# A mixer's third buffer in a ring over batches, its variances from per-batch moments, and seven landing buffers for its output

## The chip, the cores and the metric

The kernel runs on one core of one Trainium2 chip. The metric is device time in microseconds (us) of one launch, from the first to the last instruction of the core. The times before are three runs: 5021.53, 5029.39 and 5036.27 us, median 5029.39. The profile is of one further execution, with a span of 5033.2 us; all times of single instructions below are counted from the start of that span.

## The reference

The input is x with 4 images of 384 channels and 64 x 64 points, float32. Four layers follow one another, each as `x = x + layer(groupnorm(x))`: an attention, a convolution with an 8 x 8 Fourier filter and a gate, a token-and-channel mixer, and a 7 x 7 dynamic convolution. The change lies in layer 2, the mixer, and at the start of layer 3. What they compute is this, with `_bn` a batch normalization over batch and space, and `x2` the input of layer 2 after its group norm:

```python
tok = _bn(kw[:, 0:1] * y3 + kw[:, 1:2] * y5 + y1, ar_g, ar_b)
gp = tok.mean(axis=(2, 3), keepdims=True)
gates = sigmoid(_bn(_pw(gelu(_bn(_pw(gp, cg_w1), ...)), cg_w2), ...))
tok = tok * gates
h1 = gelu(_bn(_pw(tok, cm_w1), cm_g1, cm_b1))     # 384 -> 768 channels
h2 = _bn(_pw(h1, cm_w2), cm_g2, cm_b2)            # 768 -> 384 channels
x = x + gate * (tok + h2) + (1 - gate) * x2
# layer 3 begins with a group norm of x, its mean and its maximum over space:
# these give one scale per image and channel (x_w), then a 7 x 7 convolution
```

`h1` and `h2` need statistics over all four batches before the first value can be normalized. That cuts the mixer into three passes over the data: the first matrix product, the second, and the sum with which layer 3 begins.

## The kernel before

Channels lie on the 128 partitions, in three groups j = 0, 1, 2 (NJ = 3); a batch of a group is a row of 4096 points, and it is worked in four blocks of 1024. A framework places the instructions: the program is written in one order, each engine gets a queue of its own that is kept in order, waits are put in for data and for buffers, and a scheduler sets the place of each instruction in its queue.

**The first pass, "e" (in `phase_ef`, L1356 to L1403).** Sixteen blocks, b = 0 to 3 outside and i = 0 to 3 inside. For each block the token tensor is loaded in three parts, one for each channel group. Groups 0 and 1 land in a tile `e_tok` that has two buffers. Group 2 lands in a slice of `z_`, a large tile that is otherwise unused in this pass; which slice is written out by hand, at L1359:

```python
at = i % 3 * 1024
t = [t01[:, 0], t01[:, 1], self.z_[:, at : at + 1024]]
```

All loads are issued from SyncE's queue (SP), each part in four pieces. DVE scales the parts in place (L1364), TensorE forms six outputs `h_s` of 1024 columns from them (L1379, 72 matmuls a block in the trace), ACT copies them to `e_h` (L1386), DVE takes `bn_stats` of them (L1388) and works out the rest of the sum, `e_x` (L1392, L1393), of which the third part again reads the slice of `z_`. Then ACT's queue writes `e_h` to DRAM as `hid` (L1403), once per block.

**The statistics of the first product (L1404 to L1407).** After all blocks, one `bn_aggr` per output group folds the 32 sets of moments into mean and variance (L1406), and `bn_scale_shift` turns them into a scale and a shift (Ln and Exp on ACT, L312 and L313, three small DVE operations, L322 to L324). ACT's Gelu of the next pass (L1422) waits for them.

**The second pass, "f" (L1410 to L1447).** The same sixteen blocks: `hid` is loaded, Gelu is applied, TensorE forms `h_m` (L1435, 72 matmuls a block), ACT copies it out, DVE takes `bn_stats`. The result goes to DRAM as `h2`, but for the last batch, which stays in `z_` (`h2_last`). At the end of each batch a `bn_aggr` per group gives the moments of that batch alone, `mvb` (L1447); they are needed for layer 3's mean. After all blocks a second `bn_aggr` per group folds all 32 sets (L1450), and `bn_scale_shift` follows.

**`over_batches` (L327)** folds moments of four batches into one mean and variance. Before the change it is called once, for the token statistics ahead of the first pass ("ar"): `bn_stats` and `bn_aggr` for each group (L333, L334), a reduction and one more operation (L336, L338).

**The start of layer 3 (`phase_g`, `x2_of`, L1592).** The batches go in the order 3, 0, 1, 2 and the groups in the order 1, 2, 0. For each, a row of `wx` (what the first pass left of the sum) is loaded into one of three row buffers `x` (L1604), and `h2` comes in four quarters of 1024 into buffers `g_h2` (L1610); batch 3 has its rows loaded ahead and its `h2` in `z_`. For each quarter ACT scales `h2` into PSUM (`x_m`, L1614), DVE adds it to the row (L1615), ACT squares the sum for the variance, and writes the squares over the quarter's buffer, so that this instruction (L1617) is the one that frees it, and DVE takes the maximum (L1618). Groups 1 and 2 are written back to DRAM from POOL's queue (L1625); group 0 stays and is worked on. After the three groups come the group norm and the small products that give the batch's scale (`gn_pg`, `gn_pv`, `xw_m` L1636, `xw` L1646, `gx_m`). The strips and box sums of the batch before are woven in between (`first_chunk`: `to_strips` L1678 to L1695, `boxes` L1748 to L1801); they end with the write of the row to `rest` (L1801), which frees its row buffer. All buffers of `g_h2` are of the tag `toep`, of which there are four. That tag and the tag `rest`, with three buffers of the same size, belong to the convolution that comes after.

**The convolution (`conv7`, L1700 to L1731)** is then 3072 matmuls of 128 columns, with the remaining strips and boxes woven in.

Of the kernel before, what the change touches and what calls it, by code (L numbers as in the profile page):

```python
# [21 lines left out]
F32 = mybir.dt.float32  # L22
AF = mybir.ActivationFunctionType
ALU = mybir.AluOpType
AX = mybir.AxisListType

B, C, H, W = 4, 384, 64, 64
N = H * W
NJ = 3
P = 128  # L30
# [196 lines left out]
class _Builder:  # L227
# [99 lines left out]
    def over_batches(self, name, mv):  # L327

        nc = self.nc
        st = self.sm([P, NJ, 6], f"{name}_st")  # L330
        m = self.sm([P, NJ, 2], f"{name}_m")
        for j in range(NJ):
            nc.vector.bn_stats(st[:, j, :], mv[:, j, :, 0])  # L333
            nc.vector.bn_aggr(m[:, j, :], st[:, j, :])  # L334
        within = self.sm([P, NJ], f"{name}_w")
        nc.vector.tensor_reduce(within, mv[:, :, :, 1], AX.X, ALU.add)  # L336
        var = self.sm([P, NJ], f"{name}_v")
        nc.vector.scalar_tensor_tensor(var, within, 1.0 / B, m[:, :, 1], ALU.mult, ALU.add)  # L338
        return m[:, :, 0], var

    def bn_of_four(self, name, z, g, b, func, out):

# [960 lines left out]
    def phase_ef(self, strips):  # L1303
        tc, nc = self.tc, self.nc
        with ExitStack() as ctx:
# [5 lines left out]
            ep = first.enter_context(tc.tile_pool(name="e_const", bufs=1))  # L1311
# [5 lines left out]
            a, c = self.bn_scale_shift("bn_ar", *self.over_batches("ar", self.mvt), self.vec("ar_g"), self.vec("ar_b"))  # L1317
# [12 lines left out]
            mv = self.sm([P, NJ, 2], "cg2_mv")  # L1330
            for j in range(NJ):
                nc.tensor.matmul(z[:, j], lhsT=cg2[:, j * P : (j + 1) * P], rhs=gh, start=True, stop=True)
                st = self.sm([P, 6], "cg2_st")
# [17 lines left out]


            st = ep.tile([P, 6, B * 8, 6], F32, tag="h_st", name="h_st")
            sums = cp.tile([P, NJ, B, 4], F32, tag="wx_sum", name="wx_sum")
            for b in range(B):
                for i in range(4):  # L1356
                    blk = slice(i * 1024, (i + 1) * 1024)
                    t01 = io.tile([P, NJ - 1, 1024], F32, tag="tok", name="e_tok")
                    at = i % 3 * 1024  # L1359
                    t = [t01[:, 0], t01[:, 1], self.z_[:, at : at + 1024]]  # L1360
                    for j in range(NJ):
                        for q in range(4):
                            nc.sync.dma_start(t[j][32 * q : 32 * q + 32], self.tok[4 * j + q, b, :, blk])
                        nc.vector.tensor_scalar(  # L1364
                            t[j],
                            t[j],
                            self.at[:, j, b : b + 1],
                            self.ct[:, j, b : b + 1],
                            ALU.mult,
                            ALU.add,  # L1370
                        )
                    x = io.tile([P, NJ, 1024], F32, tag="x", name="e_x1")
                    nc.sync.dma_start(x, self.x1[b][:, :, blk])
                    h = hp.tile([P, 6, 1024], F32, tag="h", name="e_h")
                    for o in range(6):
                        s = self.ps("h_s")
                        for v in range(2):
                            for j in range(NJ):
                                nc.tensor.matmul(  # L1379
                                    s[:, v, :],  # L1380
                                    lhsT=w1[:, j, o * P : (o + 1) * P],
                                    rhs=t[j][:, v * 512 : (v + 1) * 512],
                                    start=j == 0,
                                    stop=j == NJ - 1,
                                )
                        nc.scalar.copy(h[:, o, :], s.rearrange("p a b -> p (a b)"))  # L1386
                        for v in range(2):
                            nc.vector.bn_stats(st[:, o, 8 * b + 2 * i + v, :], h[:, o, v * 512 : (v + 1) * 512])  # L1388
                        if o % 2:
                            j = o // 2  # L1390
                            at = lambda v: v[:, j, b : b + 1]
                            nc.vector.tensor_scalar(x[:, j], x[:, j], at(self.gx), at(self.gn), ALU.mult, ALU.add)  # L1392
                            nc.vector.scalar_tensor_tensor(  # L1393
                                x[:, j],
                                t[j],
                                self.gate[:, b : b + 1],
                                x[:, j],
                                ALU.mult,
                                ALU.add,
                                accum_out=sums[:, j, b, i : i + 1],  # L1400
                            )
                    nc.gpsimd.dma_start(self.wx[b][:, :, blk], x)
                    nc.scalar.dma_start(self.hidden[b][:, :, blk].rearrange("o p n -> p o n"), h)  # L1403
            mv = self.sm([P, 6, 2], "h_mv")  # L1404
            for o in range(6):
                nc.vector.bn_aggr(mv[:, o, :], st[:, o].rearrange("p a b -> p (a b)"))  # L1406
            a1, c1 = self.bn_scale_shift("bn_h", mv[:, :, 0], mv[:, :, 1], self.vec("cm_g1"), self.vec("cm_b1"))  # L1407


            first.close()  # L1410
# [3 lines left out]
            st2 = cp.tile([P, NJ, B * 8, 6], F32, tag="h2_st", name="h2_st")  # L1414
            mvb = cp.tile([P, NJ, B, 2], F32, tag="h2_mvb", name="h2_mvb")
            for b in range(B):
                for i in range(4):
                    blk = slice(i * 1024, (i + 1) * 1024)
                    h = hp.tile([P, 6, 1024], F32, tag="h", name="f_h")
# [5 lines left out]
                    if b == B - 1 and 0 < i:  # L1425
                        j = self.x2_order[i - 1]
                        nc.sync.dma_start(self.x2_ahead[i - 1], self.wx[b][:, j])
                    for j in range(NJ):
# [3 lines left out]
                        for v in range(2):  # L1432
                            m = self.pm("h2_m")
# [11 lines left out]
                            nc.gpsimd.dma_start(self.h2[b][:, j, blk], out)  # L1445
                for j in range(NJ):
                    nc.vector.bn_aggr(mvb[:, j, b], st2[:, j, 8 * b : 8 * b + 8].rearrange("p a b -> p (a b)"))  # L1447
            mv = self.sm([P, NJ, 2], "h2_mv")
            for j in range(NJ):
                nc.vector.bn_aggr(mv[:, j, :], st2[:, j].rearrange("p a b -> p (a b)"))  # L1450
            a2, c2 = self.bn_scale_shift("bn_h2", mv[:, :, 0], mv[:, :, 1], self.vec("cm_g2"), self.vec("cm_b2"))


            self.mean2, self.neg2 = self.coef("mean2"), self.coef("neg2")
# [1 line left out]
            for j in range(NJ):  # L1456
                nc.vector.tensor_scalar(self.gh[:, j, :], self.gate, a2[:, j : j + 1], None, ALU.mult)
                nc.vector.tensor_scalar(self.g0[:, j, :], self.gate, c2[:, j : j + 1], None, ALU.mult)
                m = self.mean2[:, j, :]
# [132 lines left out]
    def x2_of(self, b):  # L1592


        nc = self.nc
        mv = self.sm([P, NJ, 2], "gn_mv")
        mx = self.sm([P, NJ], "max")
        for j in self.x2_order:
            at = lambda v: v[:, j, b : b + 1]
            if b == B - 1:  # L1600
                x = self.x2_ahead.pop(0)
            else:
                x = self.gx_tile("x2")
                nc.sync.dma_start(x, self.wx[b][:, j])  # L1604
            var, top = self.sm([P, 4], "x2_var"), self.sm([P, 4], "x2_max")
            for q in range(4):
                sl = slice(q * 1024, (q + 1) * 1024)
                if b < B - 1:
                    h = self.gt_p.tile([P, 1024], F32, tag="toep", name="g_h2", bufs=4)
                    nc.sync.dma_start(h, self.h2[b][:, j, sl])  # L1610
                else:
                    h = self.h2_last[:, j, sl]
                m = self.psum.tile([P, 1024], F32, tag="c", name="x2_m", bufs=2)
                nc.scalar.activation(m, h, AF.Identity, bias=at(self.g0), scale=at(self.gh))  # L1614
                nc.vector.tensor_add(x[:, sl], x[:, sl], m)  # L1615

                nc.scalar.activation(h, x[:, sl], AF.Square, bias=at(self.neg2), accum_out=var[:, q : q + 1])  # L1617
                nc.vector.tensor_reduce(top[:, q : q + 1], x[:, sl], AX.X, ALU.max)  # L1618
                yield None
            nc.vector.tensor_reduce(mx[:, j : j + 1], top, AX.X, ALU.max)  # L1620
            nc.vector.tensor_copy(mv[:, j, 0:1], at(self.mean2))
            nc.vector.tensor_reduce(mv[:, j, 1:2], var, AX.X, ALU.add)
            nc.vector.tensor_scalar(mv[:, j, 1:2], mv[:, j, 1:2], 1.0 / N, None, ALU.mult)
            if j:
                nc.gpsimd.dma_start(self.scratch["x2"][b][j], x)  # L1625
        r, gm, n, _ = self.norm_of_groups(mv, True)
# [5 lines left out]
        m = self.pm("xw_m")  # L1632
# [18 lines left out]
        m = self.pm("gx_m")  # L1651
# [180 lines left out]
```

## Time and profile before

| what | before |
|---|---|
| time, median of 3 (lowest to highest) | 5029.39 us (5021.53 to 5036.27) |
| span of the profiled execution | 5033.2 us, 47996 instructions |
| TensorE busy | 4607.7 us, 92% |
| DVE busy | 2729.0 us, 54% |
| ACT busy | 2108.7 us, 42% |
| POOL busy | 762.8 us, 15% |
| DMA | 723.30 MB, mean 144 GB/s |

How to read it: TensorE is the engine that is busy nearly all of the time, so the span is mostly a row of stages that TensorE fills, with gaps in which it waits. The busy share of the whole doesn't show the gaps. The page divides the span into 40 slices of 126 us and gives each a digit for the busy share. In TensorE's row the slices that the change concerns, from 3271 us on, read first 9 throughout the two passes of the mixer (3271 to 4152 us), then 6 5 6 around the start of layer 3, and 9 again in the convolution. "idle before, releaser" in a line is the time for which the engine stood still ahead of these instructions, and what it then went on after. "SPq", "ACTq" and "POOLq" are the queues that issue DMAs; the time in such a line is that of the issue, not of the transfer.

### The profile page before, as it was taken

How to read it: one execution, taken by the hardware profiler on the slowest of the kernel's cores; microseconds unless marked ns; L12 is line 12 of the kernel's file. 1: busy time of each engine (PE TensorE's matmuls, PEld its weight loads, DVE VectorE, ACT ScalarE, POOL GpSimd, SP SyncE). 2: the span in 40 equal slices, each digit the busy share in tenths (PEclk: the TensorE clock that was granted, in tenths of full speed). 3: DMA queues.
4: the chain of work that ended last, by engine and by line, in shares of the span. 5: the costliest groups of instructions: out<-in, count | busy, mean ns of one | idle time of the engine just before them, and what ended most of it. 6: DMA issues, size and time to landing. Idle time of an engine off the chain costs nothing. (4 is left out here: it accounts for less than half of the span.)

```text
span 5033.2 us, 47996 instructions
## 1 busy us (share of the span) xinstructions
PE 4607.7 (92%) x17875; PEld 2614.2 (52%) x17875; DVE 2729.0 (54%) x4480; ACT 2108.7 (42%) x2811; POOL 762.8 (15%) x568
## 2 busy tenths in 40 slices
PE   5999999999999999999988999699999996569999
PEld 2333444334443444435467888344444443558999
DVE  5322455644656445565867778544421114767775
ACT  4444344554445444445345665311133334652320
POOL 1000000000000000000035555000000000135543
PEclk8999999999999999999989999799999997569999
DMA  5210211110111101113259999766664433757876
GB/s 167 72 48 29 84 57 60 65 59 33 68 63 65 52 32 63 63 61 100 89 162 286 290 293 296 255 239 248 238 238 150 150 134 136 255 181 229 235 214 193
DMA packets 344919, 723.30 MB, mean 144 GB/s; under 512 B 22011, under 2 KB 172390, under 8 KB 337766
## 3 DMA queue, kind: packets, MB, share of 16 engines
q1 hardware_dynamic: 283032, 477.56, 30.4%
q0 software_dynamic: 33152, 136.60, 7.2%
q10 hardware_dynamic: 28494, 105.99, 5.4%
q8 instruction: 144, 2.36, 0.2%
q14 instruction: 97, 0.79, 0.0%
HBM read 432.48 MB, written 287.57 MB: 143 GB/s over the span
## 5 line engine op out<-in xcount | busy, mean ns | idle before, releaser
L749 PE MATMUL av<-probs,vt 128*128 128x512 f32 x2048 | 964.6, 606 | 0.0
L720 ACT ACTIVATE probs<-sc_s 128x1024 f32<-128x1024 f32 x512 | 500.9, 1021 | 788.1 <-PE av L749 781.5
L749 PEld LDWEIGHTS av<-probs,vt 128*128 128x128 f32 x2048 | 370.3, 192 | 468.1 <-issue 461.0
L1154 PE MATMUL conv_m<-toep,z 128*128 128x256 f32 x2304 | 522.2, 386 | 11.0 <-DVE toep L1135 6.8
L945 DVE SCALAR_TENSOR_TENSOR acc<-band,vecs,acc 128x512 f32<-128x512 f32 x708 | 496.7, 746 | 45.8 <-POOL band L906 40.0
L1435 PE MATMUL h_m<-f_h,cm_w_t 128*128 128x512 f32 x1152 | 496.4, 594 | 7.9 <-ACT f_h L1422 7.9
L1154 PEld LDWEIGHTS conv_m<-toep,z 128*128 128x128 f32 x2304 | 440.5, 193 | 73.1 <-DVE z L1087 4.9
L1379 PE MATMUL h_s<-e_tok,cm_w_t 128*128 128x512 f32 x768 | 367.4, 602 | 5.5 <-DVE e_tok L1364 5.5
L1435 PEld LDWEIGHTS h_m<-f_h,cm_w_t 128*128 128x128 f32 x1152 | 219.4, 191 | 284.9 <-issue 273.8
L1135 POOL TENSOR_TENSOR toep<-w,band 128x1536 f32<-128x1536 f32 x94 | 323.8, 3445 | 285.7 <-PE conv_m L1154 244.7
L1722 PE MATMUL conv_m<-toep,z 128*128 128x128 f32 x3072 | 366.4, 278 | 0.1
L1722 PEld LDWEIGHTS conv_m<-toep,z 128*128 128x128 f32 x3072 | 357.1, 194 | 0.5 <-issue 0.5
L712 PE MATMUL sc_s<-q,k 32*128 32x512 f32 x2048 | 297.8, 650 | 22.5 <-ACT probs L720 22.0
L868 PE MATMUL t_m<-w_in_t,xb 128*128 128x384 f32 x768 | 276.9, 495 | 2.7 <-DVE coef L885 1.6
L1386 ACT COPY e_h<-h_s 128x1024 f32<-128x1024 f32 x96 | 97.2, 1012 | 421.4 <-PE h_s L1379 421.4
L782 PE MATMUL proj_m<-xm,w_proj_t 128*128 128x512 f32 x576 | 265.9, 600 | 5.0 <-DVE xm L735 3.5
L1379 PEld LDWEIGHTS h_s<-e_tok,cm_w_t 128*128 128x128 f32 x768 | 148.1, 193 | 192.6 <-issue 185.6
L789 DVE SCALAR_TENSOR_TENSOR x_res<-proj_m,bn_c,x_res 128x512 f32<-128x512 f32 x96 | 71.8, 748 | 319.5 <-PE proj_m L782 316.5
L1388 DVE BATCH_NORM_STATS2 h_st<-e_h 128x6 f32<-128x512 f32 x192 | 123.4, 685 | 194.9 <-ACT e_h L1386 194.9
L1443 DVE BATCH_NORM_STATS2 h_st<-f_h 128x6 f32<-128x512 f32 x72 | 49.8, 694 | 323.1 <-ACT f_h L1442 323.1
L868 PEld LDWEIGHTS t_m<-w_in_t,xb 128*128 128x128 f32 x768 | 142.7, 191 | 138.8 <-issue 59.6
L1379 PE MATMUL h_s<-z,cm_w_t 128*128 128x512 f32 x384 | 198.0, 599 | 12.6 <-DVE z L1364 12.6
(369 smaller groups left out, 6285.1 us busy)
## 6 DMA issues: line engine op xcount, KB each, us to landing
d<-d_o ACTq DMA_DIRECT2D x96, 512.0 KB
c_d<-d SPq DMA_DIRECT2D x96, 512.0 KB
hid<-e_h ACTq DMA_DIRECT2D x16, 3072.0 KB
f_h<-hid SPq DMA_DIRECT2D x16, 3072.0 KB
x_in<-in_x SPq DMA_DIRECT2D x96, 256.0 KB
x_res<-in_x SPq DMA_DIRECT2D x32, 768.0 KB
xa<-x_res POOLq DMA_DIRECT2D x32, 768.0 KB, 3.7
xa_in<-xa SPq DMA_DIRECT2D x32, 768.0 KB
```

The costliest lines, as they stand in the source:

```text
L712: nc.tensor.matmul(s[:, g], lhsT=k4[32 * g : 32 * g + 32, c], rhs=q[i][32 * g : 32 * g + 32], start=True, stop=True,)
L720: nc.scalar.activation(p[:, h * 1024 : (h + 1) * 1024], s[:, 2 * h : 2 * h + 2].rearrange("p a b -> p (a b)"), AF.Exp, scale=0.25,)
L749: nc.tensor.matmul(av, lhsT=vt[:, 4 * c + v, :], rhs=p[:, v * 512 : (v + 1) * 512], start=c == 0 and v == 0, stop=c == 7 and v == 3,)
L782: nc.tensor.matmul(m, lhsT=self.w_proj[:, j, o * P : (o + 1) * P], rhs=xm[:, j], start=j == 0, stop=j == NJ - 1,)
L868: nc.tensor.matmul(m[:, 0:C], lhsT=xb[:, j], rhs=self.w_in[:, j, :], start=j == 0, stop=j == NJ - 1,)
L945: nc.vector.scalar_tensor_tensor(out, src(j, k), w, done, ALU.mult, ALU.add)
L1135: eng.tensor_tensor(t, self.w53[:, at : at + 192].rearrange("p (m n) -> p m n", n=8).unsqueeze(2).to_broadcast([P, 24, 8, 8]), band.rearra ...
L1154: nc.tensor.matmul(m[:, c * 256 : (c + 1) * 256], lhsT=self.z_[:, at : at + P], rhs=t[:, 12 * c + 4 * i : 12 * c + 4 * i + 4].rearrange("p ...
L1379: nc.tensor.matmul(s[:, v, :], lhsT=w1[:, j, o * P : (o + 1) * P], rhs=t[j][:, v * 512 : (v + 1) * 512], start=j == 0, stop=j == NJ - 1,)
L1388: nc.vector.bn_stats(st[:, o, 8 * b + 2 * i + v, :], h[:, o, v * 512 : (v + 1) * 512])
L1435: nc.tensor.matmul(m, lhsT=w2[:, o, j * P : (j + 1) * P], rhs=h[:, o, v * 512 : (v + 1) * 512], start=o == 0, stop=o == 5,)
L1722: nc.tensor.matmul(m[:, ch * P : (ch + 1) * P], lhsT=self.z_[:, at : at + P], rhs=t[:, 8 * c + 2 * i : 8 * c + 2 * i + 2].rearrange("p m a ...
```

## The change

Three edits:

1. The slice of `z_` for the third part goes round over all sixteen blocks: `(4 * b + i) % 3` in place of `i % 3`. Before, block 3 of a batch and block 0 of the next one had the same slice, 0. Now any three blocks in a row have three different ones.
2. The mixer's statistics come from the moments of each batch. In the first pass six `bn_aggr` of 8 sets stand at the end of each batch (the new tile `hmv`), and `over_batches` folds the four batches. In the second pass the per-batch moments were there already, and `over_batches` takes the place of the `bn_aggr` over 32 sets. `over_batches` itself is rewritten: no `bn_stats` and `bn_aggr` by group, but seven small operations on all groups at once (sum, scale, difference, square, add, sum, scale). It is also used for "ar", as before.
3. The quarters of `h2` in `x2_of` alternate between the tags `toep` (four buffers) and `rest` (three): seven buffers in all.

```diff
     def over_batches(self, name, mv):
-        for j in range(NJ):
-            nc.vector.bn_stats(st[:, j, :], mv[:, j, :, 0])
-            nc.vector.bn_aggr(m[:, j, :], st[:, j, :])
-        within = self.sm([P, NJ], f"{name}_w")
-        nc.vector.tensor_reduce(within, mv[:, :, :, 1], AX.X, ALU.add)
-        nc.vector.scalar_tensor_tensor(var, within, 1.0 / B, m[:, :, 1], ALU.mult, ALU.add)
+        nc.vector.tensor_reduce(mean, mv[:, :, :, 0], AX.X, ALU.add)
+        nc.vector.tensor_scalar(mean, mean, 1.0 / B, None, ALU.mult)
+        nc.vector.tensor_sub(d, mv[:, :, :, 0], mean.unsqueeze(2).to_broadcast([P, n, B]))
+        nc.vector.tensor_mul(d, d, d)
+        nc.vector.tensor_add(d, d, mv[:, :, :, 1])
+        nc.vector.tensor_reduce(var, d, AX.X, ALU.add)
+        nc.vector.tensor_scalar(var, var, 1.0 / B, None, ALU.mult)
...
-                    at = i % 3 * 1024
+                    at = (4 * b + i) % 3 * 1024
...
-            for o in range(6):
-                nc.vector.bn_aggr(mv[:, o, :], st[:, o].rearrange("p a b -> p (a b)"))
-            a1, c1 = self.bn_scale_shift("bn_h", mv[:, :, 0], mv[:, :, 1], ...)
+                for o in range(6):
+                    nc.vector.bn_aggr(hmv[:, o, b], st[:, o, 8 * b : 8 * b + 8].rearrange("p a b -> p (a b)"))
+            a1, c1 = self.bn_scale_shift("bn_h", *self.over_batches("h", hmv), ...)
...
-            for j in range(NJ):
-                nc.vector.bn_aggr(mv[:, j, :], st2[:, j].rearrange("p a b -> p (a b)"))
-            a2, c2 = self.bn_scale_shift("bn_h2", mv[:, :, 0], mv[:, :, 1], ...)
+            a2, c2 = self.bn_scale_shift("bn_h2", *self.over_batches("h2", mvb), ...)
...
-                    h = self.gt_p.tile([P, 1024], F32, tag="toep", name="g_h2", bufs=4)
+                    tag, bufs = (("toep", 4), ("rest", 3))[q % 2]
+                    h = self.gt_p.tile([P, 1024], F32, tag=tag, name="g_h2", bufs=bufs)
```

The scheduler places some instructions otherwise as a result. On SyncE's queue the loads of a block at a batch's start stand before in the order "one piece of `e_tok`, four of `z_`, seven of `e_tok`", and after in the order of all other blocks, "eight of `e_tok`, four of `z_`". At the start of layer 3, three quarters of group 2 move ahead of the first row load of batch 0. For group 0 of batches 1 and 2, three of the four quarters (q = 0, 2, 1) stand ahead of the row load of that group, where before all four stood behind it. TensorE takes the matmuls of a batch's first output in the same order as those of all others, two of `e_tok` and one of `z` for each half, where before the four of `e_tok` came first. Apart from that, and from the added and removed small operations, TensorE, DVE, ACT and POOL keep their orders but for exchanges of near neighbours, most of them from layer 3 on.

## The prediction

> **What bounds the kernel now.** I read the page first (TensorE 92% busy), then the table of busy times for the four stretches from the mixer on:
>
> ```profile
> core 0: us, PE busy (x) PEld busy (x) DVE busy (x) ACT busy (x) POOL busy (x), PEclk, DMA share, GB/s
> 3200.90:3725.70 524.80, 504.31 (x1153) 221.75 (x1153) 261.53 (x395) 102.82 (x103) 11.47 (x16) 0.98 0.63 237
> 3725.70:4222.70 497.00, 496.39 (x1152) 219.37 (x1152) 71.62 (x108) 163.11 (x191) 19.29 (x37) 1.00 0.39 146
> 4222.70:4513.60 290.90, 149.64 (x728) 135.57 (x729) 200.22 (x371) 192.68 (x272) 62.65 (x64) 0.58 0.63 225
> 4513.60:5033.20 519.60, 485.95 (x4174) 478.82 (x4172) 370.94 (x409) 119.22 (x203) 244.99 (x148) 0.98 0.73 217
> ```
>
> The rows are pass e, pass f, the start of layer 3, and the convolution. Passes e and f run the same number of matmuls of the same shape, yet e takes 28 us more: that is what to look for. The third row is no TensorE stage (half of the time idle, clock 0.58): there a chain through all engines sets the pace. The fourth is TensorE's again and simply starts when the third ends, so what any of the first three loses or gains should reach the end.
>
> Next, where e loses. The write of `hid` is issued once per block, so its spacing is the block's time. From the timeline of ACT:
>
> ```profile
> 3297.97 0.37 ACTq L1403 DMA_DIRECT2D hid<-e_h  x1
> 3328.87 0.37 ACTq L1403 DMA_DIRECT2D hid<-e_h  x1
> 3366.39 0.37 ACTq L1403 DMA_DIRECT2D hid<-e_h  x1
> 3397.29 0.37 ACTq L1403 DMA_DIRECT2D hid<-e_h  x1
> ```
>
> A block takes 30.90 us; the one from 3328.87 on, the first of batch 1, takes 37.52. The first blocks of batches 2 and 3 take 36.64 (3459.09 to 3495.73) and 37.75 (3588.43 to 3626.18); all others 30.90. The cause is in the timelines of SP, DVE and TensorE there:
>
> ```profile
> 3327.82 1.69 SPq L1363 DMA_DIRECT2D z<-tok  x4
> 3329.56 14.08 SPq L1363 DMA_DIRECT2D e_tok<-tok  x7
> ```
>
> ```profile
> 3334.26 0.81 DVE L1364 TENSOR_SCALAR z<-z,at,ct 128x1024 f32<-128x1024 f32 x1 [4.11 <-DMA z<-tok]
> ```
>
> ```profile
> 3335.13 2.07 PE L1379 MATMUL h_s<-z,cm_w_t 128*128 128x512 f32 x2 [3.91 <-DVE z L1364]
> 3337.00 3.43 PE L1379 MATMUL h_s<-e_tok,cm_w_t 128*128 128x512 f32 x4
> ```
>
> The third part of a batch's first block can only be loaded when TensorE has done with the same slice, at the end of the block before. Its load, its scaling and a TensorE stop of 3.91 us follow; then six matmuls run at half speed (3.43 us for four, normally 1.88).
>
> For the third stretch, the group list with the scaling of `h2`, and ACT and SP around one such place:
>
> ```profile
> L1614 ACT ACTIVATE x_m<-g_h,g,gh 128x1024 f32<-128x1024 f32 x36 | 42.8, 1196 | 13.2 <-DMA g_h<-h 13.2
> ```
>
> ```profile
> 4373.66 0.32 SPq L1604 DMA_DIRECT2D x<-wx  x1
> 4374.07 5.95 SPq L1610 DMA_DIRECT2D g_h<-h  x4
> ```
>
> ```profile
> 4382.93 1.21 ACT L1614 ACTIVATE x_m<-g_h,g,gh 128x1024 f32<-128x1024 f32 x1 [3.25 <-DMA g_h<-h]
> 4387.67 1.21 ACT L1614 ACTIVATE x_m<-g_h,g,gh 128x1024 f32<-128x1024 f32 x1 [3.53 <-DMA g_h<-h]
> ```
>
> ACT waits 13.2 us in all for quarters of `h2`: 2.22 at 4290.81, the two shown, 3.00 at 4456.41 and 1.18 at 4466.11. The last four are in group 0 of batches 1 and 2, the group that ends the batch; its quarters are issued behind its row and share the DMA engines with it.
>
> **What the Trainium skill says.** "TensorE: Matmul & The Clock Gate", Part 1, states that an idle window of some 3.4 us drops the array to half its clock and that a busy one brings it back: the stops of 3.77 to 4.88 us are followed by matmuls at half rate in this trace, so a stop costs more than its idle time. "DMA: Bandwidth & Descriptors", section "Issuing engines are not separate DMA queues", says that all queues share the same 16 DMA engines: between 4374 and 4388 us a row of 2.1 MB and four quarters of 0.52 MB compete, as the 4.74 us between the two waits' ends shows. "VectorE: DVE Perf Modes", section on the TRN2 errata, says that each small operation pays a fixed cost: here dependent DVE operations on a few columns start 0.20 us apart (L322, L323, L324 at 3723.11, 3723.31, 3723.51).
>
> **The change part by part.**
>
> *The ring of `z_`.* With three different slices in a row, the load of a batch's first block may start two blocks earlier than now, as within a batch, where the trace shows no stop. The `e_tok` pieces, seven of which have stood behind that load in SP's queue, are freed as well. What is saved is the excess of the three blocks: 37.52 + 36.64 + 37.75 - 3 x 30.90 = 19.2 us. It is TensorE's own time with nothing beside it, so all of it counts. The DMA share in this stretch is 0.63, so earlier loads find room. Ends: 16 us if a smaller wait (row of `e_x`, `e_tok`) shows behind it, 19.2 if none. I take 19.2.
>
> *Statistics, pass e.* On the path are only the operations after the last `bn_stats` (3718.88, 1.28 us). Before: one `bn_aggr` of 32 sets, 1.02 us. After: one of 8 sets, 0.37 us by the row of L1447, then the seven operations of `over_batches`, each waiting for the one before, 7 x 0.20 = 1.4. So 1.77 against 1.02: +0.75 us, with ACT's Ln behind it and all of TensorE behind that. The 18 `bn_aggr` of earlier batches (18 x 0.37 = 6.7 us) lie on DVE, busy for half of this stretch; they are hidden.
>
> *Statistics, pass f.* The per-batch `bn_aggr` was there already. The last `bn_aggr` of 32 sets (0.96 us, 4223.76) goes, 1.4 us come: +0.45 us.
>
> *Statistics, "ar".* From 3184.75 to ACT's Ln at 3185.84 eight pipelined operations take 1.09 us; seven dependent ones take 1.4: +0.3 us. Sum of the three: +1.5 us. Ends: 0.8 if they start 0.1 us apart, as independent ones do in this trace, and 2.5 at 0.3 us (0.26 us is the longest of the small reductions, L1057).
>
> *Seven buffers.* Three quarters of a group ending a batch are now issued before its row, as soon as earlier quarters are squared. Then 0.52 MB instead of 2.1 MB compete with the row. Does a row get stuck behind a quarter that isn't free? In the order of the changed queue the quarter ahead of each row load needs a buffer freed by a square that also had to be done before (for example, the last one before the rows of batch 1, groups 2 and 0, needs the squares of group 1, done by 4348 us, and the row itself can't go before 4354.78). So no new wait. What may be saved: at 4290.81 about 2 us (the strips of batch 3 stand behind it on ACT). In group 0 of batch 1 the quarters are ready, and the adds (now from 4384.17 to 4395.3) are limited by the row and by ACT and DVE, about 2.3 us per quarter. With the row there at about 4381 they end at about 4391: 4 us. In batch 2, waits of 3.00 + 1.18, some of it replaced by the row's own arrival: 3 us. Sum 9 us. Bounds: 0, if the rows or DVE's queue come last everywhere, and about 16, the 13.2 us plus some gain for the rows.
>
> Sum: -19.2 + 1.5 - 9 = -26.7 us; 5029.4 - 26.7 = 5002.7, rounded to 5003 us.
>
> **The rivals.**
>
> *A, the early quarters bring nothing.* The chain of the third stretch goes through row buffers, POOL's writes and xw: DVE waits 25.6 us there for TensorE's `xw_m`, and POOL's write of a row stood behind an xw for 5.9 us. If these come last, only the ring counts: 5029.4 - 19.2 + 1.5 = 5012 us.
>
> *B, the early quarters bring more.* If each wait of 13.2 us is on the chain and rows land earlier too, 16 us or slightly more: 5029.4 - 19.2 + 1.5 - 16 = 4996 us.
>
> *C, the third stretch gets worse.* Quarters that are issued early compete with the rows that come last for two of the three batches, or an exchange of neighbours on POOL delays a write. At 5 us for each of three batches: 5012 + 15 = 5027 us, no measurable change. At double that, 5042 us, slower. For it speaks that DMA is at 0.98 in some of the 20 us windows there (4282 to 4302); against it that the bytes are the same and come out of just these windows.
>
> *D, the ring's gain is lost again*, because pass f or layer 3 wait for something other than TensorE. Against it: pass f's first Gelu waits for the last statistic of pass e, with nothing but TensorE's work ahead of it. It would give about 5020 us.
>
> **How the numbers follow.** Forecast (ring in full, 5 to 13 us from the buffers): 0.50. A: 0.22. B: 0.13. C: 0.08, of which 0.03 slower. D: 0.07. The bound of 0.3% is 15 us, so faster means below 5014: forecast, B and nearly all of A, as A is 2 us below it and the three runs before spread by 15 us: 0.50 + 0.13 + 0.20 = 0.83 and a little of D: 0.84. Slower 0.03. Same 0.13. The range takes in A and B with 3 to 6 us beyond them for the spread of medians: 4990 to 5016.
>
> **What would show it.** The spacing of `hid` in all sixteen blocks at 30.9 us, and no TensorE idle time put down to `z` in pass e, show the first step right. Pass e would then last about 506 us in place of 524.8, and the gap of TensorE between the passes, 7.88 us now, about 8.6. The stretch to the first matmul of the convolution, 290.9 us now, would be near 282 with ACT's wait for `g_h` under 3 us; at 290 with the wait gone, rival A is right. The prediction is wrong if one of the three batch starts still stops TensorE, or if the third stretch grows.

## The result, and the profile after

The changed kernel takes 5004.08 us (median of 4 runs, 5003.26 to 5010.24) against 5029.15 us before (4 runs, 5021.53 to 5036.27): the ratio is 0.9953, with a 95% interval from 0.9936 to 0.997. Five further runs of it, beside another 11 of the kernel before, gave 5011.48 us and a ratio of 0.9964 (0.995 to 0.9977). The profiled execution spans 5001.5 us, before 5033.2.

First the table of busy times by stage of the changed kernel, cut where the stages of the kernel before were cut, except that layer 3 begins with its first `x_m`: pass e, pass f with the statistics after it, the start of layer 3, the convolution.

```profile
core 0: us, PE busy (x) PEld busy (x) DVE busy (x) ACT busy (x) POOL busy (x), PEclk, DMA share, GB/s
3192.60:3697.66 505.06, 496.31 (x1152) 219.92 (x1153) 264.56 (x420) 102.80 (x103) 11.47 (x16) 0.99 0.66 246
3697.66:4200.17 502.51, 496.38 (x1152) 219.90 (x1152) 73.13 (x125) 166.09 (x196) 19.29 (x37) 0.99 0.40 148
4200.17:4472.90 272.73, 143.53 (x717) 129.04 (x718) 195.58 (x356) 188.88 (x264) 63.10 (x63) 0.59 0.65 234
4472.90:5001.50 528.60, 490.75 (x4186) 483.98 (x4184) 369.52 (x413) 119.75 (x206) 244.15 (x148) 0.97 0.72 213
```

With the same cuts the kernel before had 3200.9 us ahead of pass e, then 524.7, 502.0, 285.9 and 519.6. So in this pair of profiles 8.3 us went ahead of pass e, where hardly anything was changed, 19.7 in pass e and 13.2 at the start of layer 3; the passes' boundary costs 0.5 more, and the convolution is 9.0 us *longer*. The first of these five numbers says nothing of the change, and in those of pass e, of the start of layer 3 and of the convolution a part is chance, as the other profiles will show: one pair of executions isn't enough to read stages to a few us.

Pass e first. The writes of `hid` in the timeline of ACT, where batch 1 begins:

```profile
3319.22 0.37 ACTq L1405 DMA_DIRECT2D hid<-e_h  x1
3350.12 0.37 ACTq L1405 DMA_DIRECT2D hid<-e_h  x1
```

This is the block that took 37.52 us; it takes 30.90, and so do all others. In the list of what the engines sat idle for around `h_s`, no line with `z` is left (before, "DVE z" stood there with 27.6 us in 6 waits: three stops, each counted once for the matmul, together 12.6 us, and once for its weight load). The two waits for data that remain belong to the first block of the pass:

```profile
  DVE e_tok L1366: 6.1, 2
  DMA e_x<-x: 5.5, 1
```

The end of pass e, from DVE's timeline (start, duration, operation, and in brackets the idle time before it):

```profile
3691.34 0.37 DVE L1407 BATCH_NORM_AGGREGATE h_mv<-h_st 128x2 f32<-128x48 f32 x1
3691.75 0.18 DVE L332 TENSOR_REDUCE h_m<-h_mv 128x6 f32<-128x24 f32 x1
3691.96 0.17 DVE L333 TENSOR_SCALAR h_m<-h_m 128x6 f32<-128x6 f32 x1
3692.17 0.18 DVE L335 TENSOR_TENSOR h_d<-h_mv,h_m 128x24 f32<-128x24 f32 x1
...
3693.03 0.17 DVE L339 TENSOR_SCALAR h_v<-h_v 128x6 f32<-128x6 f32 x1
3695.09 0.17 DVE L322 TENSOR_TENSOR bn_h_a<-bn_h_a,vecs 128x6 f32<-128x6 f32 x1 [1.89 <-ACT bn_h_a L313]
```

The seven operations start 0.21 us apart. From the last `bn_aggr` to the first matmul of pass f is now 6.32 us, before 5.48; TensorE's gap between the passes is 8.72 us, where about 8.6 were foretold.

At the start of layer 3, the group of the scaling of `h2` in the list of groups:

```profile
L1614 ACT ACTIVATE x_m<-g_h,g,gh 128x1024 f32<-128x1024 f32 x36 | 42.8, 1195 | 0.0
```

ACT no longer waits for a quarter of `h2` at all; before, it was 13.2 us.

### The profile page after: what moved, and what is told of

The parts are those of the page before. It is cut to its first block, busy times and chain, and to the rows that moved or that the text cites. A ratio compares the mean times of both kernels' runs of the same rounds, so it can differ in the third digit from the quotient of the medians.

```text
span 5001.5 us, 48017 instructions
## 1 busy us (share of the span) xinstructions
PE 4589.6 (92%) x17875; PEld 2609.4 (52%) x17875; DVE 2728.0 (55%) x4508; ACT 2108.8 (42%) x2811; POOL 762.3 (15%) x568
```

## The experiments

Every run below stood beside runs of the kernel before on its chip, whose medians were 5028.14, 5028.22 and 5028.2 us. Single runs of one and the same kernel lie 7 to 26 us apart, so an edit of a few us has to be read from stages of many profiles, or from many runs.

**e1: the ring alone.**

```diff
-                    at = i % 3 * 1024
+                    at = (4 * b + i) % 3 * 1024
```

> Only the ring of the third token slice is changed. Theory 1 (the ring saves TensorE's stops at the three batch starts and nothing else): 19.2 us less than before, about 5010 us; pass e about 505 us long in place of 524.8, all blocks 30.9 us apart; the stretch from the last copy of h2 to the first matmul of the convolution and the convolution as before, 286 and 520 us, within the spread of one run to the next. Theory 2 (the gain is lost again behind it, as DMA or layer 3 wait for something else): less than 12 us. Theory 3 (the 8.3 us that the profile of the changed kernel is ahead of before when the mixer starts belong to the ring): pass e starts at about 3192 us here too.

5010.09 us, ratio 0.997 (0.996 to 0.998). All blocks take 30.90 us; pass e takes 505.4. The gain isn't lost afterwards, which answers the rival that it would be. What to compare it with is shown by the kernels that have no ring: their pass e took 524.7 us (before), 521.2 (e2) and 519.3 (e3), so the stops cost less in other executions than in the profile of before. Here the idle list around `h_s` of e3, the stops in place:

```profile
  DVE z L1364: 23.5, 6
  DMA hid<-e_h: 11.7, 1
```

23.5 us, where before had 27.6, counted in the same double way (TensorE itself stood still for 10.5 us and 12.6). In nine profiles with the ring pass e took 504.2 to 506.5 us, mean 505.5. The means differ by 16.2 us.

**e2: the statistics alone** (`over_batches`, the batch-wise `bn_aggr` of pass e, and the two calls, as in the change).

> Only the statistics are changed. Theory 1: 1.5 us more, that is no difference that can be measured; in the trace 0.8 us more between the last write of hid and the first matmul of pass f, 0.5 us more between the last copy of h2 and the first use of its scale, 0.3 us more ahead of the token scale. Theory 3 (the 8.3 us before the mixer come with the new small tiles or the new operations): 8 us less, with pass e starting at about 3192 us. If the start of pass e lies anywhere between 3190 and 3203 us without a pattern over these runs, the 8.3 us are the spread of code that the change doesn't touch.

5028.55 us, ratio 0.9998 (0.9989 to 1.0007): not to be told from no change. The chain is there all the same: 6.32 us from the last `bn_aggr` to pass f, as in each of the profiles with this edit that I read, and 5.48 in each without it.

**e3: the seven buffers alone.**

```diff
-                    h = self.gt_p.tile([P, 1024], F32, tag="toep", name="g_h2", bufs=4)
+                    tag, bufs = (("toep", 4), ("rest", 3))[q % 2]
+                    h = self.gt_p.tile([P, 1024], F32, tag=tag, name="g_h2", bufs=bufs)
```

> Only the seven buffers are added. Theory 1 (the stretch before the convolution gets shorter by some 13 us, and the convolution then takes some 9 us longer since its own loads and strips aren't there earlier): 4 us less than before, about 5025 us; the stretch about 273 us, the convolution about 528 us. Theory 2 (the longer convolution in the changed kernel's profile is chance): 13 us less, about 5016 us; the stretch 273 us, the convolution 520 us. Theory 3 (the shorter stretch is chance): no change, 286 and 520 us.

5025.24 us, ratio 0.9993 (0.9983 to 1.0003). The waits for `h2` are gone, the stretch to the first matmul of the convolution is 278.6 us, and the convolution takes 524.3. Pass e starts at 3202.0 us, so the 8.3 us ahead of it were not this edit's. The time, 2.9 us below its neighbours' median, is nearest to theory 1, but by itself it can't be told from no change.

**e4: ring and statistics, four buffers.**

> The changed kernel without the seven buffers. Theory 1: 17.7 us less than before, about 5011 us, with the stretch before the convolution at 286 us and the convolution at 520 us; the seven buffers are then worth about 4 to 7 us in the changed kernel. Theory 2 (the buffers bring their 13 us in full): the changed kernel is faster than this one by 13 us.

5011.3 us, ratio 0.9964 (0.9953 to 0.9976); pass e starts at 3199.9 us, and the start of layer 3 takes 286.5, as before. Theory 1's sum was right; the changed kernel is not 13 us faster than this one, so theory 2 falls.

**e5: the changed kernel again, unaltered.**

> The changed kernel again, unaltered, so that it stands beside the other runs on the same chip. Where the convolution's 48 sums are timed from the first x_m of layer 3, the four profiles without the seven buffers reach the fifth sum 348.7 to 354.7 us (spread 6) and the last at 797.9 to 803.3; the two with them at 343.7 and 348.7, and 796.3 and 797.8. Theory 1: the buffers are worth 4 to 5 us at the end and about 5 at the fifth sum; the 13 us of the first profile were partly chance. Then this profile has the fifth sum at 343 to 349 and the last at 794 to 799, and the median is 5003 to 5009 us. Theory 2: the first profile is typical, 9 us are won before the convolution and given back in it each time: fifth sum at 343 to 345, last at 796 to 797, median 5002 to 5005. Pass e starts anywhere from 3192 to 3203 (untouched code) under both.

5011.48 us. The fifth sum comes at 348.4 us, the last at 801.6 (the four profiles named there read 347.3 to 353.3 at the fifth). Theory 2 falls, since the first profile was not typical; theory 1's place for the fifth sum was met, its last sum and its median were missed by some 3 us on the slow side.

**e6: ring and seven buffers, old statistics.**

> Ring and seven buffers, the statistics as before. Theory 1 (the seven dependent operations stand on the path at two places that stop TensorE and once in the U-net): the gap from the last bn_aggr's start to pass f's first matmul is 5.48 us again (6.32 with the change), the one from the last aggr group to x_m 4.9 (5.5), and the time is 1 to 2 us below the changed kernel's, too little to be told from it by the medians. Theory 2 (aggregating by batch takes 18 operations off DVE's end and gains something elsewhere): the time is equal or 1 to 3 us longer.

5004.74 us, ratio 0.9958 (0.9945 to 0.9971). The chain is 5.48 us again. The times of e5 and e6 (5011.48 and 5004.74, 5 and 6 runs) can't be told apart by their ranges, 5004.96 to 5017.02 and 5000.28 to 5015.56.

**e7: the convolution's write of its sums one group later**, to see whether the order in SP's queue eats the head start.

```diff
         nc.vector.tensor_add(of, of, m)
-        nc.sync.dma_start(self.out[j][:, c0 : c0 + 8], o)
+        self.late = (self.out[j][:, c0 : c0 + 8], o)
...
         nc.sync.dma_start(o, self.rest[j][c0 : c0 + 8].rearrange("c y b n -> (y b) c n"))
+        self.write_late()
```

> The changed kernel with each write of the convolution's sums issued one group later, behind the next group's two loads, so that the strips' loads on SP's queue no longer stand behind a write that waits for DVE's sum of the same group. Theory 1 (what the convolution gives back is lost where TensorE waits for strips, and these stand in SP's queue behind the write): SP's wait for rest_o, 128 us in all, falls below 40, TensorE's waits for z, 20 us, fall below 8, and the time is 8 to 15 us below the changed kernel's. Theory 2 (the loads are paced by the DMA engines, at 0.8 to 0.94 there, and the queue's order is of no matter): the strips' loads take as much longer as they start earlier; the time is within 3 us.

5006.36 us, ratio 0.9956 (0.9943 to 0.997). SP's waits in the first 400 us of the convolution (line waited for, us in total, times, longest) of e7:

```profile
SPq L1702 <- DVE rest_o L1738: 119.2, 20, 11.2
```

They are nearly what they were (128.1 us in the changed kernel): SP simply arrives at the later write earlier and waits there. TensorE's waits for `z` stay too, at 20.3 us (20.5 in the changed kernel). Theory 1 falls.

**e8: the late write with the four buffers.**

> Ring and statistics with the four old buffers, and the late write of the sums. Theory 1 (the queue's order eats part of the head start): with the late write the seven buffers are worth more than without it, 7 to 10 us between this kernel and the one with late write and seven buffers, against some 5 without it. Theory 2 (the head start is lost to the DMA engines or was chance): 3 to 5 us between the two, as without it.

5011.22 us, ratio 0.9963 (0.995 to 0.9976): 4.9 us above e7, as theory 2 had it.

**e9: each box result written to `rest` in two pieces** (on e6: ring, seven buffers, old statistics).

```diff
+            if part == 3:
+                nc.gpsimd.dma_start(*rows(0, 24))
             for q in range(2):
...
-                nc.gpsimd.dma_start(self.rest[j][:, :, b], x.rearrange("p (y n) -> p y n", n=P))
+                nc.gpsimd.dma_start(*rows(24, 32))
```

> Ring and seven buffers with the old statistics (the kernel of e6), and each box result written to rest in two pieces, three quarters as soon as they are summed and the last quarter at the end, in place of 2.1 MB at the end. Theory 1 (what the convolution gives back is the wait of its first sum for the reload of rest, which stands behind the write of the last box result of the chunk: DVE waits 4.5 to 4.7 us there in every profile with the seven buffers and 1.8 in every one with four, SP 8.4 us for the write): the write that SP waits for falls from 8.4 to about 3 to 4 us, DVE's wait to under 1, TensorE's 4.2 us for the first sum go, the second sum comes 3 to 5 us earlier after the first x_m than in e6 (309.9) or its mean with seven buffers (313.6), and the time is 2 to 5 us below e6's. Theory 2 (the first sum waits for the DMA engines in general): the wait stays within 1 us and the time within 2 us.

4997.87 us, ratio 0.9936 (0.992 to 0.9952), five runs from 4989.58 to 5001.44: the fastest kernel of the study, below the changed one's 5004.08 and 5011.48. How it gains is only partly as theory 1 said. SP's wait for the write falls from 8.4 to 5.4 us, not to 3 or 4; DVE's wait for the reload is gone; but TensorE still waits 3.5 us for the first sum, and the second sum is only 0.6 us earlier than in e6. DVE's timeline of e9 ahead of that sum (L1731) shows why:

```profile
4502.21 3.65 DVE L1775 SCALAR_TENSOR_TENSOR box<-edge,off,box 128x128 f32<-128x128 f32 x1
4505.78 0.61 DVE L1776 SCALAR_TENSOR_TENSOR box<-in_x,off,box 128x384 f32<-128x384 f32 x1
...
4510.48 1.21 DVE L1710 TENSOR_TENSOR toep<-wmix,band_p 128x1024 f32<-128x1024 f32 x1
4511.61 1.21 DVE L1731 TENSOR_TENSOR rest_o<-rest_o,conv_m 128x1024 f32<-128x1024 f32 x1
```

The sum waits for no event: it stands in DVE's own queue behind box operations, one of which took ten times its usual 0.34 us. With the reload early, DVE became what comes last. From the convolution's first matmul to the third sum TensorE stands idle for 5.5 us, against 7.8 to 8.9 in the five profiles with seven buffers and whole writes. These 2.6 us below their mean are all of the gain that the traces place. The edit splits every box result's write, those inside the convolution too, and the profile of e9 reaches the end 795.1 us after the first `x_m`, that of e6 after 797.0: where the rest of the gain in the times comes from isn't shown.

**e10: the same write with the ring alone, four buffers.**

> The same writes in two pieces with the ring alone, four buffers (the kernel of e1). Theory 1: here DVE waits only 1.8 us for the reload and TensorE not at all, so the second sum moves by 1 to 2 us and the time by 0 to 2; the seven buffers are worth 2 to 4 us more between this kernel and e9 than the 3.8 us that they are worth without the split (all runs so far, fitted together). Theory 2: the two differ by some 4 us, as without the split.

5005.34 us, ratio 0.9956 (0.994 to 0.9971), nine runs from 4991.45 to 5017.88. At the medians this is 4.8 us below e1, and e9 is 6.9 below e6; the seven buffers are worth 7.5 us with it and 5.3 without (e1 to e6). The direction is that of theory 1, but runs of e10 spread over 26 us, and so this difference of differences is not shown. With the split TensorE waits 3.5 us for the first sum, as in e9, where e1 has no such wait. Its idle time from the first matmul to the third sum is 5.6 us, as without the split (5.4 to 5.9 in the five profiles with four buffers), and the profile reaches the end 804.9 us after the first `x_m`, e1's after 802.9. So in this pair of traces the split gains nothing, where the medians differ by 4.8 us.

**All runs together.** A least-squares fit over the 145 runs of the eleven kernels (62 of them of the kernel before), with one number for each edit, which assumes that edits add up and that chips agree. The second column is one standard error; single runs scatter by 5.9 us around the fit.

| edit | us | +- |
|---|---|---|
| ring of `z_` | -16.7 | 1.4 |
| statistics | -0.4 | 1.4 |
| seven buffers | -4.5 | 1.2 |
| late write (e7, e8) | -0.4 | 2.2 |
| `rest` in two pieces (e9, e10) | -7.5 | 2.1 |

Both kernels with `rest` in two pieces ran on one chip only, where the kernel before had a mean some 1.5 us lower than elsewhere. The three edits of the change sum to -21.6 us, so 5006.5 from the fit's 5028.1. The nine runs of the changed kernel have a mean of 5008.6.

## Why the prediction was right, point by point

The forecast was 5003 us, out of -19.2, +1.5 and -9. The mechanisms hold but for one, that what the start of layer 3 gains reaches the end whole, and two of the three sizes were too large.

*The ring: right.* Its marks were met exactly: 30.90 us in every block, no idle time for `z`, 505.1 us where about 506 were foretold. The size is the excess of the three blocks in *one* execution, the longest pass e of the three without a ring. Over profiles it is 16.2 us, over runs 16.7 +- 1.4: within the ends given (16 to 19.2), at the lower one.

*The statistics: right by the trace, too small for the clock.* Pass e to f +0.84 (foretold +0.75); from pass f's last `bn_stats` to `x_m` +0.54 (+0.45; 5.48 us for 4.94). The term for "ar", +0.3, can't be isolated: pass e starts at 3193.0 to 3202.0 us in six profiles without the new `over_batches` (mean 3197.6) and at 3192.6 to 3200.6 in six with it (mean 3197.6). The same numbers show that the 8.3 us ahead of pass e in the first pair of profiles are spread between executions. The sum, 1.4 us on the path as far as traced, isn't contradicted by -0.4 +- 1.4 in the times.

*The seven buffers: right before the convolution, twice too large at the end.* The waits for `h2` went as foretold. (The account of what shares the DMA engines between 4374 and 4388 us left out a row that POOL's queue writes there: 1.56 of the 4.85 MB moved were that queue's.) I compared five profiles with four buffers (before, e1, e2, e4, e8) with five with seven (after, e3, e5, e6, e7). Each batch is measured from its predecessor's `gx_m` matmul to its own:

| us, mean | four | seven | gained | foretold |
|---|---|---|---|---|
| batch 0 | 66.4 | 61.6 | 4.8 | 2 |
| batch 1 | 69.4 | 66.4 | 3.0 | 4 |
| batch 2 | 71.7 | 68.2 | 3.5 | 3 |
| first `x_m` to the first conv matmul | 284.8 | 274.7 | 10.1 | 9 |
| first `x_m` to the landing of the last box result in `rest` | 314.9 | 307.5 | 7.4 | |
| first `x_m` to the second sum of the convolution | 321.0 | 313.6 | 7.4 | |
| first `x_m` to the third sum | 329.7 | 323.8 | 5.9 | |
| first `x_m` to the end | 806.6 | 801.3 | 5.3 | |

Batches 1 and 2 differ in every pair of profiles. Batch 0 has two lengths on either side, about 67 or 61.5 us with four and 65 or 58 to 60 with seven; which of them comes changes from one execution to the next. The two lengths go with TensorE's granted clock (PEclk, the third number from the right) from 28 to 42 us after the `gx_m` before, where DVE waits for `box_m` matmuls. Here this stretch and DVE's wait in it, of e4 (long) and of e1 (short):

```profile
4294.50:4308.50 14.00, 11.08 (x47) 9.48 (x46) 9.78 (x16) 7.36 (x12) 1.28 (x1) 0.50 0.40 121
DVE x L1796 <- PE box_m L1794: 4.5, 4, 1.8
```

```profile
4289.70:4303.70 14.00, 9.64 (x69) 8.88 (x69) 13.47 (x29) 10.65 (x16) 1.28 (x1) 0.90 0.46 140
DVE x L1797 <- PE box_m L1795: 0.4, 1, 0.4
```

In all six long ones of the ten profiles the clock was at one half throughout these 14 us (a `box_m` matmul took 421 ns in the median), in all four short ones it was full for 7.6 to 11.3 us of them (275 or 276 ns). Why the clock rises there in some executions only isn't shown. Like compared with like, seven buffers win 2.9 us where batch 0 is long (67.7 to 64.8) and 2.0 where it is short (61.5 to 59.5), close to the 2 foretold; the rest of the 4.8 is that four of five were long with four buffers and two of five with seven. Of the 13.2 us of the first pair of profiles, 7.7 are a short batch 0 against a long one.

The step that failed is one that I didn't write as a step: "simply starts when the third ends, so what any of the first three loses or gains should reach the end". Of 10.1 us won at the first matmul, 2.7 are gone by the second sum and 4.2 by the third. DVE's and TensorE's waits in the first 100 us around the start of the convolution, of the changed kernel:

```profile
DVE rest_o L1730 <- DMA rest_o<-rest: 4.5, 1, 4.5
PE conv_m L1722 <- DVE rest_o L1730: 4.2, 1, 4.2
```

and of e1, with four buffers, where TensorE has no such line:

```profile
DVE rest_o L1730 <- DMA rest_o<-rest: 1.9, 1, 1.9
```

The first sums add `rest`, which is reloaded from DRAM after the last box result of the chunk has been written, and TensorE can't begin a third group before a sum has freed one of two PSUM buffers. In all ten profiles the first sum starts 4.1 to 4.4 us after that write has landed, so it gains what the write gains, 7.4 us, and not 10.1. DVE's wait is 4.5 to 4.7 us in all five profiles with seven buffers and 0.9 to 2.3 in the five with four, and TensorE's wait for the first sum 4.2 to 4.6 us against at most 0.1.

The mark has moved as well. Between the last `gx_m` and the convolution's first matmul TensorE runs 20 `ht_m` and 32 `box_m` with four buffers and 16 and 24 with seven; the other twelve come after that matmul, which therefore looks earlier than the work is. From it to the third sum TensorE is idle for 5.7 us with four buffers and 8.1 with seven, and busy for 39.2 and 41.0: these two differences, 2.4 and 1.8, are the 4.2 us. From the third sum to the end it is 476.9 and 477.5 us, a difference far below the spread of single profiles (474.1 to 479.8), so the rest of the convolution gives nothing back that can be seen. Of the 9.0 us that the convolution was longer in the first pair, 4.8 are the difference of the means (526.6 and 521.8), and the rest is chance: the kernel before had the shortest of all convolutions in its profile, 519.6 us, where e1, e2, e4 and e8, with its four buffers, took 521.9 to 522.6. By times the buffers are worth 4.5 +- 1.2 us, half of the 9.

*The rivals.* A, the early quarters bring nothing, would have left 5012 us; e4, which is the change without them, took 5011.3, so that sum came out, its ring too large by 2.5 us and its statistics by 2; and the fit puts the buffers' 4.5 us more than three standard errors from nothing. B is out: 16 us were not even won before the convolution. C, a worse third stretch, did not come: it shortened with seven buffers in every batch mean. D is answered by e1.

So the forecast's nearness to the first 5004 us owes something to luck: about 2.5 us of the ring and 4.5 of the buffers were overestimated, some 2 of the statistics the other way, and the median of the first four runs happened to lie 4.5 us under the mean of all nine.

## What to carry to other kernels

A ring of buffers that restarts its index at every outer iteration puts two neighbours into one buffer; counting through costs nothing and here was worth three quarters of the gain. A stage that TensorE fills doesn't pass on a head start by itself: look at what its first results need besides TensorE, here a write and a reload of `rest`, for that is the next wait. Writing that data in two pieces took off 7.5 +- 2.1 us in the times, though the traces place only 2.6 us of it, and those with seven buffers alone. And price a stop from several executions: the excess in one profile was 19.2 us, over all 16 to 17. Where a stage has two lengths, look at the granted clock before crediting an edit.

## What the runs showed of the hardware

A running POOL instruction can stop DVE. In e9 a box sum of 128 x 128 on DVE, 0.34 us in most of its executions, started at 4502.21 and took 3.65, to 4505.86, while these ran on POOL:

```profile
4501.98 1.42 POOL L1767 TENSOR_TENSOR box<-in_x 128x576 f32<-128x576 f32 x1
4503.35 2.36 POOL L1710 TENSOR_TENSOR toep<-wmix,band 128x1024 f32<-128x1024 f32 x1
```

The second ended at 4505.71. The Trainium skill, "SBUF — State Buffer", section "Who interferes with whom", says that DVE and GpSimd share one pair of ports, held for a whole instruction, and that a DVE operation with two inputs in SBUF contends with GpSimd's reads: the ends, 0.15 us apart, agree with that, and so do the twelve traces taken together. This box sum, whose two tensor inputs lie in SBUF, stands in them 432 times. 58 started while a tensor operation on POOL had at least 0.45 us left to run, and all 58 took longer, 0.67 to 3.84 us. Of the 69 that took longer than 0.45 us, 68 ended 0.14 to 0.165 us after a POOL operation ended. DVE's operations with one of two inputs in PSUM (the sums of `conv_m`, of `box_m`, and `toep` from `band_p`) started 778 times in the same situation, and none took over 1% longer than its median. No run moved the POOL operation to test it. Such a stop counts as busy time of DVE, not as a wait, and only the duration gives it away.

And the code ahead of pass e, untouched but for one short chain, took between 3192.6 and 3202.0 us from one execution to the next, though the medians of three sets of 33, 11 and 14 runs of the kernel before agreed within 0.1 us.
